# The end of a four-layer mixture-of-experts kernel: last LayerNorm and gates without Exp and Ln, gates of two batches at once, last experts placed between the batches' tails

## The chip, the cores and the metric

The kernel runs on one core of a Trainium2 chip, in one launch. The time is device microseconds from launch to end. Three runs are shown; beside them one execution was recorded by the hardware profiler, and all durations and positions below are from that one.

A core has TensorE (PE in the profile: matrix products, with weight loads shown apart as PEld), VectorE (DVE), ScalarE (ACT: activation functions, also copies), GpSimd (POOL), SyncE (SP, which here only starts transfers) and DMA queues. Each engine has its own list of instructions and waits for others by semaphores.

## The reference, cut to what matters

The input `x` is 4 batches of 512 tokens of 128 numbers. Four layers follow, each of an attention to a context of 32 tokens and a feed-forward part, each on a LayerNorm without gain. The change concerns the last feed-forward part (layer 3), and the LayerNorm ahead of it:

```python
def _L3_ffn_ref(x, router_w, w1, b1, w2, b2):
    TOP_K = 2
    xf = x.reshape(-1, D)
    logits = xf @ router_w.T                       # 8 experts
    probs = jax.nn.softmax(logits, axis=-1)
    top_v, top_i = jax.lax.top_k(probs, TOP_K)
    gates = top_v / (jnp.sum(top_v, axis=-1, keepdims=True) + 1e-09)
    out = jnp.zeros_like(xf)
    for e in range(E):
        ge = jnp.sum(jnp.where(top_i == e, gates, 0.0), axis=-1, keepdims=True)
        h = jax.nn.gelu(xf @ w1[e] + b1[e], approximate=False)
        out = out + ge * (h @ w2[e] + b2[e])
    return out.reshape(B, S, D)
...
x = x + _L3_xattn_ref(_layernorm(x, axis=-1), ctx_1024, mask_BxS2_ff1, ...)
x = x + _L3_ffn_ref(_layernorm(x, axis=-1), ...)
```

Every token goes through all 8 experts, weighted by its gates (zero for six of them). The hidden width is 256.

## The kernel before, in words

All data of the tail stays on the chip: `X[g]` is batch g, 128 partitions by 4 blocks of 128 numbers (block j holds tokens 128 j to 128 j + 127). Everything is float32. A product of 128 x 128 weights with 128 or 512 columns shows as two matmul records in the trace.

The program is written as Python generators, one chain for each batch. `together` (L110) starts the chains two steps apart and takes one step of each in turn, so that instructions of the batches are interleaved; a planner under it then orders what each engine gets by when it expects operands to be there. On the chip each engine works through that list.

The last stage, in `l3_ffn` (L1103 on), for each batch g:

1. `combine2(g)` (L1065, L1071) adds the outputs of layer 2's experts to `X[g]`.
2. `attend3(g)` normalises (`normed`, with its scaling on ACT, L219), transposes on PE (L233, the copy out of PSUM is L235), makes scores (L385), the maximum and the subtraction on DVE (L370, L371), the exponential on ACT (L372), a transpose (L398, its copy L400), the product with the values (L404), the division (L413, L414), and the output projection (L245), which is added to `X[g]` (L457). There are four blocks of scores a batch, 16 in all.
3. `route3(g)` (the chain in `routed`, L557) normalises `X[g]`: mean and variance on DVE (L192, L193), `v = variance + eps` (L195), `y = exp(-0.5 ln v)` on ACT (L197, L198), one Newton step on DVE (L202, L203, L205), the scaling on DVE (L223). Then come the transposes into `xnT[g]` (L233, L235), the product with the router's weights (L564) and the copy of the logits to SBUF (L570).
4. `gate(g)` finds the two largest logits (`argmax`, L582 to L589, twice), takes two exponentials on ACT (L1115, L1116) and makes the gates by small DVE operations (L1119 to L1131).

All chains run to their end first. Then a loop over the batches does the experts: the gates are transposed (L1138), copied (L1140) and multiplied with the second biases (L245, with `gT`), which is added to `X[g]`; for each of the 8 experts two hidden halves of 128 x 512 (L1146), Gelu on ACT (L1147), eight products back (L1151), and four DVE operations that add the gated result to `X[g]` (L1161). `X[g]` is then written out.

Hidden tiles `hT` have two buffers[...]. The tables of ACT's functions are loaded in sets: `exp_ln_tables` (L180) asks for one with Exp and Ln (L182); the load ahead of the Gelus is put in by the build (it shows at L1147). `fetch` loads this layer's weights early (L1230, L1231).

Of the kernel before, what the change touches and what calls it, by code (L numbers as in the profile page):

```python
# [8 lines left out]
F32 = mybir.dt.float32  # L9
# [58 lines left out]
def tile_kernel(ctx: ExitStack, tc: tile.TileContext, I, out):  # L68
# [115 lines left out]
        queued.close()  # L184
        queued.enter_context(tc.issue_after(load.ins))

    def moments(src, p=P, n=NJ):

        st = sm.tile([P, n, 6], F32, tag=f"st{n}", name="st")
        mv = sm.tile([P, n, 2], F32, tag=f"mv{n}", name="mv")  # L190
        for j in range(n):
            nc.vector.bn_stats(st[:p, j, :], src[:, j, :])  # L192
            nc.vector.bn_aggr(mv[:p, j, :], st[:p, j, :])  # L193
        v = small(n, "v")[:p]
        nc.vector.tensor_scalar(v, mv[:p, :, 1], EPS, None, ALU.add)  # L195
        y = small(n, "y")[:p]
        nc.scalar.activation(y, v, AF.Ln)  # L197
        nc.scalar.activation(y, y, AF.Exp, scale=-0.5)  # L198
        yield

        t = small(n, "t")[:p]
        nc.vector.tensor_tensor(t, y, y, ALU.mult)  # L202
        nc.vector.scalar_tensor_tensor(t, t, -0.5, v, ALU.mult, ALU.mult)  # L203
        r = small(n, "r")[:p]
        nc.vector.scalar_tensor_tensor(r, t, 1.5, y, ALU.add, ALU.mult)  # L205
        return mv[:p], r

    def normed(src, tag, plus=0.0, act=False, p=P, n=NJ, bufs=B, pool=wk):

        mv, r = yield from moments(src, p, n)  # L210
        y = pool.tile([P, n, D], F32, tag=tag, name=tag, bufs=bufs)
        if plus or act:
            c = small(n, "c")[:p]
            nc.vector.scalar_tensor_tensor(c, mv[:, :, 0], -1.0, r, ALU.mult, ALU.mult)
            if plus:
                nc.vector.tensor_scalar(c, c, plus, None, ALU.add)
        for j in range(n):
            if act:
                nc.scalar.activation(y[:p, j, :], src[:, j, :], AF.Identity, bias=c[:, j : j + 1], scale=r[:, j : j + 1])  # L219
            elif plus:  # L220
                nc.vector.tensor_scalar(y[:p, j, :], src[:, j, :], r[:, j : j + 1], c[:, j : j + 1], ALU.mult, ALU.add)
            else:
                nc.vector.tensor_scalar(  # L223
                    y[:p, j, :], src[:, j, :], mv[:, j, 0:1], r[:, j : j + 1], ALU.subtract, ALU.mult
                )
        yield
        return y
# [134 lines left out]
        nc.scalar.copy(vw[:rows], pt[:rows])  # L362
        return vw

    def softmax_terms(e, src, nh, n):

        e3 = e.rearrange("p (h n) -> p h n", n=n)
        src3 = src.rearrange("p (h n) -> p h n", n=n)
        mx = small(nh, "mx")
        nc.vector.tensor_reduce(mx, src3, AX.X, ALU.max)  # L370
        nc.vector.tensor_tensor(e3, src3, bc(mx, 2, n), ALU.subtract)  # L371
        nc.scalar.activation(e, e, AF.Exp)  # L372
        return e3

    def attend(xT, keys, values, g, H, n):
# [6 lines left out]
        for j0 in range(0, NJ, npb):  # L382
# [8 lines left out]
                )  # L391
            yield
            e = wk.tile([P, 512], F32, tag="att", name="att", bufs=B)
            softmax_terms(e, pt, npb * H, n)
            yield
            pt = psum()
            for k in range(4):
# [150 lines left out]
        return chain  # L548


    def routed(tag, w, bias=None, copies=()):


        xn, xnT = [None] * B, [None] * B
        logits = rk.tile([P, NT, NEXP], F32, tag=f"L{tag}", name="logits")

        def chain(g):  # L557
            xn[g] = yield from normed(X[g], "xn")
            for xd in copies:
                nc.sync.dma_start(xd[g * S : (g + 1) * S].rearrange("(j p) d -> p j d", p=P), xn[g])  # L560
            xnT[g] = yield from transposed(xn[g])
# [538 lines left out]
        return chain  # L1100


    def l3_ffn(xnT, logits, f3w1, f3w2, before, fetch):  # L1103
        gates = [None] * B

        def gate(g):
            L = logits[:, g * NJ : (g + 1) * NJ, :]
            m1, oh1 = argmax(L, NJ)
            m2, oh2 = argmax(without(L, oh1, NJ), NJ)

            z = rt.tile([P, NJ, NEXP], F32, tag="z", name="z", bufs=2)
            nc.vector.tensor_tensor(z, L, bc(m1, 2, NEXP), ALU.subtract)
            p2 = rt.tile([P, NJ], F32, tag="p2", name="p2", bufs=B)
            nc.vector.tensor_tensor(p2, m2, m1, ALU.subtract)
            nc.scalar.activation(z, z, AF.Exp)  # L1115
            nc.scalar.activation(p2, p2, AF.Exp)  # L1116
            yield
            p1 = rt.tile([P, NJ], F32, tag="p1", name="p1", bufs=B)
            nc.vector.tensor_reduce(p1, z, AX.X, ALU.add)  # L1119
            nc.vector.reciprocal(p1, p1)  # L1120
            nc.vector.tensor_tensor(p2, p2, p1, ALU.mult)
            den = rt.tile([P, NJ], F32, tag="den", name="den", bufs=2)
            nc.vector.scalar_tensor_tensor(den, p1, 1e-9, p2, ALU.add, ALU.add)
            nc.vector.reciprocal(den, den)
            nc.vector.tensor_tensor(p1, p1, den, ALU.mult)
            nc.vector.tensor_tensor(p2, p2, den, ALU.mult)
            gates[g] = rt.tile([P, NJ, NEXP], F32, tag="gates", name="gates", bufs=B)
            nc.vector.tensor_tensor(gates[g], oh1, bc(p1, 2, NEXP), ALU.mult)
            second = rt.tile([P, NJ, NEXP], F32, tag="second", name="second", bufs=2)
            nc.vector.tensor_tensor(second, oh2, bc(p2, 2, NEXP), ALU.mult)  # L1130
            nc.vector.tensor_tensor(gates[g], gates[g], second, ALU.add)  # L1131
            yield

        together([*(queue(before(g), gate(g)) for g in range(B)), fetch], 2)
        for g in range(B):
            pt = psum()
            for j in range(NJ):
                nc.tensor.transpose(pt[:NEXP, j * P : (j + 1) * P], gates[g][:, j, :], ident)  # L1138
            gT = ex.tile([NEXP, S], F32, tag="gT", name="gT", bufs=2)
            nc.scalar.copy(gT, pt[:NEXP])  # L1140
            add_to(X[g], proj(gT, f3b2, k=NEXP), X[g])
            for e in range(NEXP):
                hT = ex.tile([P, 2, S], F32, tag="hT", name="hT", bufs=2)
                for f in range(2):
                    pt = psum()
                    nc.tensor.matmul(pt, lhsT=f3w1[:, e, f * P : (f + 1) * P], rhs=xnT[g], start=True, stop=True)  # L1146
                    nc.scalar.activation(hT[:, f, :], pt, AF.Gelu, bias=col["f3_b1"][:, 2 * e + f : 2 * e + f + 1])  # L1147
                pt = psum().rearrange("p (j d) -> p j d", j=NJ)
                for j in range(NJ):
                    for f in range(2):  # L1150
                        nc.tensor.matmul(  # L1151
                            pt[:, j, :],
                            lhsT=hT[:, f, j * P : (j + 1) * P],
                            rhs=f3w2[:, e, f, :],
                            start=f == 0,
                            stop=f == 1,
                        )
                for j in range(NJ):
                    xj = X[g][:, j, :]
                    ge = gates[g][:, j, e : e + 1]  # L1160
                    nc.vector.scalar_tensor_tensor(xj, pt[:, j, :], ge, xj, ALU.mult, ALU.add)  # L1161
            nc.sync.dma_start(out[g].rearrange("(j p) d -> p j d", p=P), X[g])

    exp_ln_tables()
    xd0 = dram.tile([NTOK, D], F32, tag="xd0", name="xd0")
# [54 lines left out]
    with tc.tile_pool(name="lx", bufs=1) as lx:  # L1220
# [2 lines left out]
        attend3 = l3_xattn(*many3)  # L1223
        f3w1 = moe.tile([P, NEXP, 256], F32, tag="w1", name="f3w1")
        f3w2 = moe.tile([P, NEXP, 2, D], F32, tag="w2", name="f3w2")
        route3, _, xnT, L = routed(3, wide["router"])
        with tc.tile_pool(name="rt3", bufs=1) as rt, tc.tile_pool(name="ex3", bufs=1) as ex:

            def fetch():
# [1 line left out]
                nc.sync.dma_start(f3w2, I["f3_w2"].rearrange("e (c p) d -> p e c d", p=P))  # L1231
                yield

            l3_ffn(xnT, L, f3w1, f3w2, lambda g: queue(combine2(g), attend3(g), route3(g)), fetch())

# [168 lines left out]
```

## Time and profile before

| | us |
|---|---|
| median of 3 runs | 702.5 (698.09, 702.5, 703.27) |
| the profiled execution | 670.1 |
| its span, first to last instruction | 668.3 |

| engine | busy in the span |
|---|---|
| PE | 506.9 us (76%) |
| DVE | 330.6 us (49%) |
| ACT | 239.9 us (36%) |
| POOL | 164.3 us (25%) |

| stretch of the span | what runs |
|---|---|
| up to 456.5 us | layers 0 to 2 |
| 456.5 to 516.7 | adding layer 2's experts, layer 3's attention (last exponential ends 516.72) |
| 516.7 to 541.7 | last projections, last LayerNorm, router, gates |
| 541.7 to 668.3 | the 32 experts, writing out |

Timeline lines give start and duration in us, engine, line of the kernel, operation, what is written and read with shapes, how many instructions were merged into the line, and in brackets how long the engine stood idle before and who released it. In the table of stretches each engine has its busy time and number of instructions; PEclk is the granted clock of TensorE as a share of the full one. The chain of waits is the run of work that ended last, followed back from the end. Times of PE are partly modelled: matmuls overlap, and the end of one is an estimate.

### The profile page before, as it was taken

The page shows a single profiled execution, that of the slowest core. Times are in us where ns is not written, and L with a number is a line of the kernel's source. Part 1 is how long each engine was busy: PE and PEld are TensorE (multiplying, and loading weights), DVE is VectorE, ACT ScalarE, POOL GpSimd, SP SyncE. Part 2 cuts the span into 40 slices and gives each one's busy share as a digit, 9 for nine tenths or more (in the row PEclk, how much of TensorE's full clock was granted, in tenths as well). Part 3 has the DMA queues.
Part 4 walks back from the last instruction along what each step waited for, and adds up shares of the span by engine and source line. Part 5 has one row for each costly group of instructions (what it writes and reads, how often), then busy time and mean ns, then how long its engine had stood idle before and what let it go on. Part 6 is the DMA issues. An engine that isn't in the chain of part 4 may idle for free.

```text
span 668.3 us, 8842 instructions
## 1 busy us (share of the span) xinstructions
PE 506.9 (76%) x3047; PEld 387.0 (58%) x3047; DVE 330.6 (49%) x1378; ACT 239.9 (36%) x539; POOL 164.3 (25%) x203
## 2 busy tenths in 40 slices
PE   3658988425667968887635999950699699999996
PEld 2557765324655633676523887840377566776765
DVE  4686556352368740566681322115877843333322
ACT  2354655400225721334211333321555333333342
POOL 4244234304422100200006777772100000000000
PEclk9889989855958988997565999995799869999999
DMA  8900001291390007300202111345000000000000
GB/s 325 313 27 18 16 17 49 63 314 32 127 299 2 1 0 253 127 1 1 63 1 42 53 53 49 56 140 179 0 1 1 1 0 2 17 0 17 1 17 16
DMA packets 42990, 44.97 MB, mean 67 GB/s; under 512 B 5161, under 2 KB 31026, under 8 KB 42818
## 3 DMA queue, kind: packets, MB, share of 16 engines
q1 hardware_dynamic: 39442, 36.20, 16.5%
q0 software_dynamic: 3072, 6.30, 3.7%
q10 hardware_dynamic: 432, 1.92, 0.8%
q8 instruction: 24, 0.39, 0.2%
q14 instruction: 20, 0.16, 0.1%
HBM read 34.97 MB, written 9.44 MB: 66 GB/s over the span
## 4 chain that ended last, share of the span: by engine, by line
PE 48%; DVE 10%; POOL 7%; issue 6%; DMA 5%; ACT 4%; SPq 1%; POOLq 0%; DVEq 0%; ACTq 0%
PE pt L1151 9%; PE pt L1146 9%; PE pt L1037 4%; PE pt L1045 3%; POOL yd L689 3%; PE po L404 3%; PE pt L385 3%; PE pt L233 3%; DMA yd<-ye,to 2%; PE pt L916 2%; POOL xg L680 2%; PE pt L452 2%; PE pt L564 2%; PE pt L398 1%; PE pt L245 1%
## 5 line engine op out<-in xcount | busy, mean ns | idle before, releaser
L1151 PEld LDWEIGHTS pt<-f3w,hT 128*128 128x128 f32 x512 | 65.6, 191 | 33.4 <-ACT hT L1147 19.0
L1161 DVE SCALAR_TENSOR_TENSOR x<-pt,gates,x 128x128 f32<-128x128 f32 x128 | 36.0, 344 | 83.1 <-PE pt L1151 83.1
L1147 ACT ACTIVATE hT<-pt,cols 128x512 f32<-128x512 f32 x64 | 44.0, 688 | 73.8 <-PE pt L1146 73.5
L1151 PE MATMUL pt<-f3w,hT 128*128 128x128 f32 x512 | 68.2, 276 | 0.9 <-ACT hT L1147 0.6
L1146 PE MATMUL pt<-xnT,f3w 128*128 128x512 f32 x128 | 67.0, 612 | 0.0
L233 PE MATMUL pt<-cst,xn 128*128 128x128 f32 x96 | 25.0, 359 | 43.9 <-ACT xn L219 24.7
L680 POOL DMA_INDIRECT xg<-xd,inv x48 | 46.7, 972 | 44.5 <-DMA e_wg<-in_e_wg 16.4
L1040 ACT ACTIVATE hT<-pt 128x384 f32<-128x384 f32 (+1 forms) x64 | 27.9, 438 | 75.0 <-PE pt L1037 73.6
L689 POOL DMA_INDIRECT yd<-ye,to x48 | 46.9, 976 | 25.4 <-DVE ye L749 12.9
L233 PEld LDWEIGHTS pt<-cst,xn 128*128 128x128 f32 x96 | 15.3, 164 | 55.0 <-ACT xn L219 30.0
L192 DVE BATCH_NORM_STATS2 st<-x 128x6 f32<-128x128 f32 x128 | 32.3, 271 | 23.7 <-POOL x L545 17.6
L1045 PEld LDWEIGHTS pt<-f2w,hT 128*128 128x128 f32 x320 | 39.6, 191 | 3.3
L1037 PE MATMUL pt<-exT,f2w 128*128 128x256 f32 (+1 forms) x128 | 39.0, 448 | 2.6 <-DVE exT L713 2.6
L1045 PE MATMUL pt<-f2w,hT 128*128 128x128 f32 x320 | 40.4, 279 | 0.0
L235 ACT COPY xnT<-pt 128x512 f32<-128x512 f32 x40 | 23.2, 586 | 41.5 <-PE pt L233 41.1
L1052 DVE COPY ye<-pt 128x384 f32<-128x384 f32 (+1 forms) x16 | 7.9, 492 | 59.2 <-PE pt L1045 32.5
L398 PE MATMUL pt<-cst,att 128*128 128x128 f32 x128 | 20.5, 282 | 12.6 <-ACT att L372 12.6
L1037 PEld LDWEIGHTS pt<-exT,f2w 128*128 128x128 f32 x128 | 23.8, 197 | 10.7 <-DVE exT L713 2.8
L372 ACT ACTIVATE att<-att 128x512 f32<-128x512 f32 x32 | 20.0, 631 | 26.4 <-DVE att L371 26.1
L197 ACT ACTIVATE y<-v 128x4 f32<-128x4 f32 (+1 forms) x45 | 9.2, 203 | 53.5 <-DVE v L195 53.3
L385 PE MATMUL pt<-keys,xnT 128*128 128x256 f32 (+1 forms) x64 | 26.7, 523 | 0.9 <-ACT xnT L235 0.9
L370 DVE TENSOR_REDUCE mx<-pt 128x16 f32<-128x512 f32 (+1 forms) x32 | 21.7, 682 | 11.2 <-PE pt L385 11.0
(297 smaller groups left out, 1035.7 us busy)
## 6 DMA issues: line engine op xcount, KB each, us to landing
e_wg<-in_e_wg SPq DMA_DIRECT2D x8, 512.0 KB, 7.9
e_w<-in_e_w SPq DMA_DIRECT2D x8, 512.0 KB, 7.0
yg<-yd SPq DMA_DIRECT2D x12, 256.0 KB, 4.6
f0w<-in_f_w SPq DMA_DIRECT2D x1, 2048.0 KB, 13.2
yd<-zero SPq DMA_DIRECT2D x8, 256.0 KB, 3.4
ew<-in_e_w SPq DMA_DIRECT2D x8, 256.0 KB, 4.0
xd<-xn SPq DMA_DIRECT2D x8, 256.0 KB, 2.2
f2w<-in_f_w SPq DMA_DIRECT2D x1, 2048.0 KB, 8.3
```

What stands on the lines that cost most here:

```text
L192: nc.vector.bn_stats(st[:p, j, :], src[:, j, :])
L233: nc.tensor.transpose(pt[:, j * P : (j + 1) * P], src[:, j, :], ident)
L385: nc.tensor.matmul(pt[:, j * nk : (j + 1) * nk], lhsT=xT[:, (j0 + j) * P : (j0 + j + 1) * P], rhs=keys, start=True, stop=True,)
L680: nc.gpsimd.indirect_dma_start(out=dst, out_offset=None, in_=table[:], in_offset=bass.IndirectOffsetOnAxis(ap=idx, axis=0))
L689: ins = nc.gpsimd.indirect_dma_start(out=table[:], out_offset=bass.IndirectOffsetOnAxis(ap=to[:, c, e : e + 1], axis=0), in_=y, in_offset=None
L1037: nc.tensor.matmul(pt[:, : m * P], lhsT=f2w1[:, e, f * P : (f + 1) * P], rhs=xT, start=True, stop=True)
L1040: nc.scalar.activation(hT[:, f, : m * P], pt[:, : m * P], AF.Gelu)
L1045: nc.tensor.matmul(pt[:, c * D : (c + 1) * D], lhsT=hT[:, f, c * P : (c + 1) * P], rhs=f2w2[:, e, f, :], start=f == 0, stop=f == 3,)
L1146: nc.tensor.matmul(pt, lhsT=f3w1[:, e, f * P : (f + 1) * P], rhs=xnT[g], start=True, stop=True)
L1147: nc.scalar.activation(hT[:, f, :], pt, AF.Gelu, bias=col["f3_b1"][:, 2 * e + f : 2 * e + f + 1])
L1151: nc.tensor.matmul(pt[:, j, :], lhsT=hT[:, f, j * P : (j + 1) * P], rhs=f3w2[:, e, f, :], start=f == 0, stop=f == 1,)
L1161: nc.vector.scalar_tensor_tensor(xj, pt[:, j, :], ge, xj, ALU.mult, ALU.add)
```

## The change

- The LayerNorm in `route3` is called with `tables=False`: the first guess of the inverse root comes from an integer shift and subtraction on DVE, followed by three Newton steps in place of one. It is also called with `act=True`: the scaling is done on ACT, with a bias computed on DVE, instead of on DVE.
- `gate` works on two batches at once and waits until both have been routed. It takes one tanh in place of the two exponentials: exp(z) = (1 + t) / (1 - t) with t = tanh(z / 2).
- The table with Gelu (and tanh) is asked for once, by `after_exps`, which orders it behind the last attention exponential of every batch; tanh and Gelus are ordered behind it.
- The experts are a chain of their own, `experts()`, in the same `together` as the batches. It goes on once a batch's gates exist and all batches have left the attention. The bias product comes after the first expert of a batch instead of before it.

```diff
-    def moments(src, p=P, n=NJ):
+    def moments(src, p=P, n=NJ, tables=True):
...
-        y = small(n, "y")[:p]
-        nc.scalar.activation(y, v, AF.Ln)
-        nc.scalar.activation(y, y, AF.Exp, scale=-0.5)
-        yield
-
-        t = small(n, "t")[:p]
-        nc.vector.tensor_tensor(t, y, y, ALU.mult)
-        nc.vector.scalar_tensor_tensor(t, t, -0.5, v, ALU.mult, ALU.mult)
-        r = small(n, "r")[:p]
-        nc.vector.scalar_tensor_tensor(r, t, 1.5, y, ALU.add, ALU.mult)
+        if tables:
+            y = small(n, "y")[:p]
+            nc.scalar.activation(y, v, AF.Ln)
+            nc.scalar.activation(y, y, AF.Exp, scale=-0.5)
+            yield
+        else:
+
+            i = small(n, "i", I32)[:p]
+            nc.vector.tensor_scalar(i, v.bitcast(I32), 1, None, ALU.logical_shift_right)
+            nc.vector.tensor_scalar(i, i, -1.0, float(0x5F3759DF), ALU.mult, ALU.add)
+            y = i.bitcast(F32)
+
+        for _ in range(1 if tables else 3):
+            t = small(n, "t")[:p]
+            nc.vector.tensor_tensor(t, y, y, ALU.mult)
+            nc.vector.scalar_tensor_tensor(t, t, -0.5, v, ALU.mult, ALU.mult)
+            r = small(n, "r")[:p]
+            nc.vector.scalar_tensor_tensor(r, t, 1.5, y, ALU.add, ALU.mult)
+            y = r
...
-        nc.scalar.activation(e, e, AF.Exp)
+        exps[g] = nc.scalar.activation(e, e, AF.Exp)
...
-            xn[g] = yield from normed(X[g], "xn")
+            xn[g] = yield from normed(X[g], "xn", act=act, tables=tables)
...
+        def chain(g):
+            yield from before(g)
+            attended.append(g)
+            yield from route(g)
+            told.append(g)
+
+        def gate(g0):
+
+            while g0 + 1 not in told:
+                yield
+            n = 2 * NJ
+            L = logits[:, g0 * NJ : g0 * NJ + n, :]
+            m1, oh1 = argmax(L, n)
+            m2, oh2 = argmax(without(L, oh1, n), n)
...
+            nc.vector.tensor_tensor(z[:, :, :NEXP], L, bc(m1, 2, NEXP), ALU.subtract)
+            nc.vector.tensor_tensor(z[:, :, NEXP], m2, m1, ALU.subtract)
+            t = rt.tile([P, n, NEXP + 1], F32, tag="tanh", name="tanh", bufs=2)
+            with after_exps():
+                nc.scalar.activation(t, z, AF.Tanh, scale=0.5)
+            yield
+            nc.vector.tensor_scalar(z, t, -1.0, 1.0, ALU.mult, ALU.add)
+            nc.vector.reciprocal(z, z)
+            nc.vector.scalar_tensor_tensor(z, t, 1.0, z, ALU.add, ALU.mult)
...
+        def after_exps():
+
+            stack = ExitStack()
+            if not load:
+                with ExitStack() as behind:
+                    for g in range(B):
+                        behind.enter_context(tc.issue_after(exps[g].ins))
+                    load.append(nc.scalar.preload_act_table_set("gelu_and_others"))
+            stack.enter_context(tc.issue_after(load[0].ins))
+            return stack
...
+        def experts():
+            for g in range(B):
+                while gates[g] is None or len(attended) < B:
+                    yield
+                for e in range(NEXP):
+                    if e == 1:
+                        second_biases(g)
+                    expert(g, e)
+                    yield
+                nc.sync.dma_start(out[g].rearrange("(j p) d -> p j d", p=P), X[g])
+
+        together(
+            [*(chain(g) for g in range(B)), fetch, gate(0), gate(2), experts()],
+            late={g: 2 * g for g in range(B)} | {B: 2 * B, B + 1: 0, B + 2: 0, B + 3: 0},
+        )
...
-        route3, _, xnT, L = routed(3, wide["router"])
+        route3, _, xnT, L = routed(3, wide["router"], act=True, tables=False)
```

`expert(g, e)` and `second_biases(g)` hold the instructions of the old loop unchanged, with each Gelu issued under `after_exps()`.

## The prediction

> **What bounds the kernel now.** I read the page first (TensorE, PE, is busy 76% and holds 48% of the chain of waits; its two largest lines are the last experts, L1151 and L1146), then the busy time by stretch over the end, then the timeline of each engine between the last attention block and the first expert. Only that end is edited.
>
> ```profile
> core 0: us, PE busy (x) PEld busy (x) DVE busy (x) ACT busy (x) POOL busy (x), PEclk, DMA share, GB/s
> 514.60:528.20 13.60, 9.82 (x77) 8.51 (x75) 11.79 (x72) 4.58 (x13) 0.00 (x0) 1.00 0.00 1
> 528.20:541.70 13.50, 9.43 (x37) 7.21 (x37) 10.07 (x79) 3.93 (x12) 0.00 (x0) 0.50 0.00 1
> 541.70:548.20 6.50, 6.50 (x24) 3.78 (x24) 2.01 (x12) 2.73 (x4) 0.00 (x0) 0.72 0.00 0
> 548.20:668.30 120.10, 114.58 (x654) 81.19 (x652) 37.89 (x131) 43.59 (x64) 0.00 (x0) 1.00 0.03 10
> ```
>
> From 548.2 us on PE is full at full clock: 3.51 us for an expert (its blocks of 14 L1151 matmuls start at 553.53, 557.04 and 560.54 in the chain), 30.37 us for a batch. Nothing there changes. From 514.6 to 541.7 PE waits for a third of the time, and in the second half its clock (PEclk) is halved. The PE timeline of that part:
>
> ```profile
> 513.58 1.02 PE L385 MATMUL pt<-keys,xnT 128*128 128x512 f32 x2
> 514.44 1.05 PE L245 MATMUL pt<-w,oT 128*128 128x128 f32 x8
> 515.33 1.06 PE L404 MATMUL po<-v,aT 128*128 128x128 f32 x8
> 517.33 0.30 PE L233 MATMUL pt<-cst,xn 128*128 128x128 f32 x1 [0.94 <-DVE xn L223]
> ...
> 525.23 1.16 PE L245 MATMUL pt<-w,oT 128*128 128x128 f32 x8 [0.45 <-ACT oT L235]
> 528.52 1.15 PE L233 MATMUL pt<-cst,xn 128*128 128x128 f32 x4 [2.12 <-DVE xn L223]
> 530.34 2.08 PE L564 MATMUL pt<-w,xnT 128*128 128x128 f32 x8 [0.68 <-ACT xnT L235]
> ```
>
> Eight matmul records take 1.05 us before the clock drops and 2.08 us after. On ScalarE (ACT):
>
> ```profile
> 516.09 0.63 ACT L372 ACTIVATE att<-att 128x512 f32<-128x512 f32 x1 [1.33 <-DVE att L371]
> ...
> 540.86 0.21 ACT L1116 ACTIVATE p<-p 128x4 f32<-128x4 f32 x1 [1.09 <-DVE p L1114]
> 541.08 1.28 ACT L1147 ACT_TABLE_LOAD   x1
> 543.80 0.69 ACT L1147 ACTIVATE hT<-pt,cols 128x512 f32<-128x512 f32 x1 [1.44 <-PE pt L1146]
> ```
>
> The last attention exponential ends at 516.72, but 14 small exponentials and logarithms of this tail (0.2 us each) follow, so the Gelu table is loaded at 541.08. It costs nothing there: the first Gelu waits for PE.
>
> [...]
>
> **The change part by part.** Profiled execution: 670.1 us (span 668.3).
>
> *LayerNorm.* Per batch, Ln and Exp go (2 x 0.20 us on ACT); 2 integer operations, 6 more Newton steps and one bias (L214 kind) are added on VectorE (DVE), 0.15 us each. Dependent ones start 0.2 us apart (L1121, L1123, L1124 at 536.23, 536.45, 536.64), so the variance-to-scale chain goes from about 1.5 to 2.6 us. The scaling moves from DVE (4 in 1.06 us) to ACT (4 in 1.65 us, as the L219 row).
>
> *Gates.* Two batches at once: 4 x 23 small DVE operations become 2 x 26, 8 small activations become 2 tanh (some 0.26 us). It saves 40 x 0.1 us of DVE, but batch 0's gates now wait for batch 1's logits.
>
> *Table load.* It stands right behind the 16th exponential, 1.28 us, ahead of batch 0's scaling on ACT.
>
> *Order.* The program as built puts on PE: the last score matmul, then the transposes of batch 0's normed rows, and only between and behind these batch 1's output projection, the 15th value product, batch 0's router. Before, that projection and product ran at 514.44 to 516.39 and needed none of this. On DVE each batch's logits copy stands ahead of the next batch's whole norm. Of the experts, one (batch 0's first) lies ahead of batch 3's norm on PE and ACT. No DMA is added; SP's order and POOL's are the same.
>
> The walk, with rows above (PE at half clock 0.21 us a record in a dense stretch, 32 in 7.19 at L452; full 0.11):
>
> 1. Scores end 514.6; maximum, subtraction, exponential (0.69, 0.69, 0.63, with the new small ones between): 516.8. Load: 518.1. Scaling of batch 0: 518.1 to 519.75; first transpose 518.65. PE has stood 4.0 us, so I take its clock as halved (a 2.1 us pause in thin work, 526.4 to 528.5, did it before).
> 2. Transposes with batch 1's projection (12 records) to 521.5, 15th product to 523.2; clock back; router of batch 0 to 524.1. Before: 520.2.
> 3. Logits at 524.3, then 14 dependent DVE steps: batch 1's scale at 527.4, scaling to 529.05. PE meanwhile has 0.9 us of transposes and stands 3 us: half clock. Transposes and batch 2's projection to 530.5, 16th product to 532.2, router to 533.9. Before: 524.8.
> 4. Logits 534.2; 31 interleaved operations at 0.1 us, 3.4 in all: batch 2's scale at 537.6. Same pattern: router of batch 2 to 542.5. Before: 532.4.
> 5. First expert, 2 L1146 products, 3.2 us (1.7 full, 3.7 half clock): 545.7. Its Gelus end 546.5, then batch 3's scaling (its scale is ready at 546.2) to 548.2, beside PE's 16 L1151 records, to 548.2.
> 6. Transposes, gate transposes, copy, bias product: 550.4. Second expert to 554.5, with batch 3's router inside. Third to 559.1.
>
> Before, the third expert's last block ends at 553.53 + 1.56 = 555.1. From there on the order is the same, so the change costs 559.1 - 555.1 = **4.0 us**: 674.1 against 670.1. The median of the runs shown, 702.5, lies 32 above the profiled execution, for no reason that the trace shows; in proportion 4.0 becomes 4.2: **706.7, say 707**.
>
> The gain is there: an expert is done before batch 3's router. It is eaten by the three serial rounds of 9 us (before: 4.6, 7.6 and 5.7 from router to router), in which PE waits for DVE and then runs at half clock.
>
> **Unknown sizes.** [...] Spacing of dependent DVE operations over three chains of 14: 0.03 either way is 1.3 us. Clock at each round: the rivals. Integer shift and multiply: 0.14 us for a 128x16 int32 row (L631), so nothing else is hidden.
>
> **Rivals.**
> - *Half clock throughout* (slower). In 530 to 541 PE was busy more than half of the time and the clock stayed at 0.50. If that holds from 518 to 550, with 2.08 us for each group of eight, the walk puts the routers' ends at 526.1, 537.1 and 546.6 (rounds of 10 to 11 us) and the third expert's at 564.1: +9.0 us[...]. [...]
> - *Full clock throughout.* Routers end at 522.5, 529.9 and 537.4 (rounds of 7.4 us), the third expert at 553.2: -1.9, 700.6. For it: the clock survived pauses of 3 us at 36 to 39 and 206 to 209 us. Against: 4.0 us is longer.
> - *The overlap does what the words say* (faster). Tails keep the old pace, the first expert and the bias fill PE's pauses, and the second expert follows batch 3's router at 538.2: at half clock (3.7 + 1.7 us) it ends at 543.6 instead of 551.6 (the block at 550.03 + 1.56): -8, 694.5. It needs PE not to wait at 514.6, against the built order.
> - *It hardly overlaps at all.* The order shows one expert of 32 ahead of batch 3's router, so a gain of more than an expert and its cold start (541.7 to 548.1, 6.4 us, plus 2 for the bias) is excluded; this caps the rival above.
>
> **How the numbers follow.** Forecast 0.45, half clock 0.33, full clock 0.12, overlap 0.08, rest 0.02. One per cent is 7.0 us, about what runs from 698.09 to 703.27 can tell from no change. Forecast, own range +1.5 to +8 (704 to 711): a fifth beyond +7. Slower: 0.30 of the half-clock case, 0.09 of the forecast, 0.01: 0.40. Faster: 0.08. Within: 0.52. Range: 698 to 715, which leaves out the overlap and the ends of the others.
>
> **What would show it.** In the changed profile: the load right behind the last exponential near 517; PE idle some 4 us from 514.6, released by the scaled rows; PEclk 0.50 soon after; router to router about 9 us; the third expert's end near 559. Wrong if PE does not stand at 514.6, if rounds take under 7 us, or if any time moves ahead of 510 us, where no instruction changes.

## The result: 0.4% slower, and the profile after

| | kernel before | changed kernel |
|---|---|---|
| median of 20 runs each, us | 700.44 (695.71 to 703.27) | 703.20 (699.50 to 708.03) |
| ratio, 95% interval | | 1.0040 (1.0022 to 1.0059) |
| the profiled execution, us | 670.1 | 704.2 |
| its span, us | 668.3 | 702.4 |
| start of the last score product to start of the last block of expert products, us | 148.29 | 150.72 |

The change costs 2.8 us by the runs. The two profiled executions differ by 34 us, but 31.65 of these lie ahead of the last score product (513.58 us before, 545.23 after), where no instruction changed; the last section returns to that. I therefore compare the last row, called **the tail** from here on: two starts of the PE timeline subtracted (before: 661.87 - 513.58; after: 695.95 - 545.23). It grew by 2.43 us. To set a position of the changed kernel beside the prediction, take 31.65 off.

The table of stretches over the first three of the four parts shown before, each moved by 31.65 us:

```profile
core 0: us, PE busy (x) PEld busy (x) DVE busy (x) ACT busy (x) POOL busy (x), PEclk, DMA share, GB/s
546.25:559.85 13.60, 6.82 (x39) 6.33 (x39) 7.37 (x37) 6.01 (x12) 0.00 (x0) 0.75 0.00 0
559.85:573.35 13.50, 8.97 (x55) 8.00 (x55) 9.85 (x61) 4.53 (x11) 0.00 (x0) 0.75 0.00 1
573.35:579.85 6.50, 5.60 (x36) 3.85 (x35) 3.43 (x19) 4.08 (x8) 0.00 (x0) 1.00 0.01 3
```

In the first stretch PE is busy for 6.82 us instead of 9.82 and issues 39 records instead of 77. Its clock is worse than before (0.75 against 1.00). In the second and third the clock is better (0.75 and 1.00, against 0.50 and 0.72), and part of the loss comes back. The PE timeline shows where PE stands:

```profile
545.23 1.02 PE L396 MATMUL pt<-keys,xnT 128*128 128x512 f32 x2
550.37 0.86 PE L242 MATMUL pt<-cst,xn 128*128 128x128 f32 x2 [4.11 <-ACT xn L228]
551.02 0.64 PE L254 MATMUL pt<-w,oT 128*128 128x128 f32 x2
...
554.86 1.20 PE L575 MATMUL pt<-w,xnT 128*128 128x128 f32 x8
...
559.61 0.33 PE L242 MATMUL pt<-cst,xn 128*128 128x128 f32 x1 [2.67 <-ACT xn L228]
...
561.89 1.10 PE L575 MATMUL pt<-w,xnT 128*128 128x128 f32 x8
...
567.96 0.86 PE L242 MATMUL pt<-cst,xn 128*128 128x128 f32 x2 [4.53 <-ACT xn L228]
...
570.75 1.77 PE L575 MATMUL pt<-w,xnT 128*128 128x128 f32 x8
572.35 1.88 PE L1179 MATMUL pt<-xnT,f3w 128*128 128x512 f32 x4
```

Three pauses, of 4.11, 2.67 and 4.53 us, each ended by the scaled rows of a batch (`xn`, L228). The routers (L575) of batches 0 to 2 start at 554.86, 561.89 and 570.75: 7.0 and 8.9 us apart. Batch 1's output projection (L254, from 551.02) stands behind the first pause, though its operand `oT` had been copied by 545.59 (ACT L244, 545.00 + 0.59); before the change it started 0.86 us after the last score product. ScalarE shows what batch 0's rows waited for:

```profile
547.88 0.63 ACT L383 ACTIVATE att<-att 128x512 f32<-128x512 f32 x1 [1.80 <-DVE att L382]
548.52 1.28 ACT L1171 ACT_TABLE_LOAD   x1
549.82 1.65 ACT L228 ACTIVATE xn<-x,c,r 128x128 f32<-128x128 f32 x4
```

The last exponential, the load and the scaling follow each other without a gap.

### The profile page after: what moved, and what is told of

It reads as the page before. It is cut to its first block, busy times and chain, and to the rows that moved or that the text cites. A ratio compares the mean times of both kernels' runs of the same rounds, so it can differ in the third digit from the quotient of the medians.

```text
span 702.4 us, 8820 instructions
## 1 busy us (share of the span) xinstructions
PE 523.1 (74%) x3047; PEld 399.9 (57%) x3047; DVE 332.1 (47%) x1358; ACT 242.4 (35%) x541; POOL 164.2 (23%) x203
## 4 chain that ended last, share of the span: by engine, by line
PE 44%; DVE 12%; issue 7%; POOL 6%; ACT 4%; DMA 4%; another core or an unknown queue 3%; SPq 1%; POOLq 0%; DVEq 0%; ACTq 0%
PE pt L1185 8%; PE pt L1179 8%; POOL yd L700 4%; PE pt L1056 3%; PE pt L1048 3%; PE po L415 3%; PE pt L396 3%; PE pt L242 3%; PE pt L927 2%; DVE st L192 2%; POOL xg L691 2%; PE pt L865 2%; PE pt L463 1%; PE pt L409 1%
## 5 line engine op out<-in xcount | busy, mean ns | idle before, releaser
L1185 PE MATMUL pt<-f3w,hT 128*128 128x128 f32 x512 | 68.6, 277 | 1.3 <-ACT hT L1181 0.9
L1179 PE MATMUL pt<-xnT,f3w 128*128 128x512 f32 x128 | 64.9, 597 | 0.0
L242 PE MATMUL pt<-cst,xn 128*128 128x128 f32 x96 | 27.9, 382 | 45.5 <-ACT xn L228 31.1
L1051 ACT ACTIVATE hT<-pt 128x384 f32<-128x384 f32 (+1 forms) x64 | 26.4, 439 | 102.0 <-PE pt L1048 43.4
L1056 PE MATMUL pt<-f2w,hT 128*128 128x128 f32 x320 | 45.1, 296 | 21.9 <-ACT hT L1051 16.0
L1056 PEld LDWEIGHTS pt<-f2w,hT 128*128 128x128 f32 x320 | 42.7, 205 | 27.1 <-ACT hT L1051 17.0
L242 PEld LDWEIGHTS pt<-cst,xn 128*128 128x128 f32 x96 | 16.8, 180 | 58.5 <-ACT xn L228 37.0
L244 ACT COPY xnT<-pt 128x512 f32<-128x512 f32 x40 | 23.2, 585 | 43.7 <-PE pt L242 43.4
L409 PE MATMUL pt<-cst,att 128*128 128x128 f32 x128 | 22.1, 299 | 11.6 <-ACT att L383 11.6
L228 ACT ACTIVATE xn<-x,c,r 128x128 f32<-128x128 f32 x64 | 26.5, 483 | 11.1 <-DVE c L225 7.2
L396 PE MATMUL pt<-keys,xnT 128*128 128x256 f32 (+1 forms) x64 | 28.5, 554 | 0.9 <-ACT xnT L244 0.9
L415 PEld LDWEIGHTS po<-v,aT 128*128 128x128 f32 x192 | 26.2, 209 | 4.9 <-issue 3.3
```

The lines of the kernel that those rows point to most:

```text
L242: nc.tensor.transpose(pt[:, j * P : (j + 1) * P], src[:, j, :], ident)
L396: nc.tensor.matmul(pt[:, j * nk : (j + 1) * nk], lhsT=xT[:, (j0 + j) * P : (j0 + j + 1) * P], rhs=keys, start=True, stop=True,)
L415: nc.tensor.matmul(po[:, k, :], lhsT=aT[:, k * P : (k + 1) * P], rhs=of(values[k % nch], cols + hpc, g), start=True, stop=True,)
L1056: nc.tensor.matmul(pt[:, c * D : (c + 1) * D], lhsT=hT[:, f, c * P : (c + 1) * P], rhs=f2w2[:, e, f, :], start=f == 0, stop=f == 3,)
L1185: nc.tensor.matmul(pt[:, j, :], lhsT=hT[:, f, j * P : (j + 1) * P], rhs=f3w2[:, e, f, :], start=f == 0, stop=f == 1,)
```

## The experiments

The prediction's reason is that the order, not the work, costs the time: batch 1's projection was built in behind batch 0's transposes, which made the rounds serial. One difference in the code could do that. The old LayerNorm suspended its chain (`yield`) between Exp and the Newton step; the new branch has no such point, so that a batch's scaling and transposes are emitted one turn earlier, ahead of the next batch's projection. The rivals were the longer chain on VectorE, the half clock, ScalarE's scaling behind the table load, and the gates of two batches.

All runs together (the ratio is to the kernel before, run beside them):

| run | what differs | tail, us | PEclk | ratio (95% interval) |
|---|---|---|---|---|
| kernel before | | 148.29 | 0.83 | 1 |
| changed kernel | as in the result | 150.72 | 0.86 | 1.0040 (1.0022 to 1.0059) |
| after_again | the changed kernel again | 150.65 | 0.90 | 1.0038 (1.0015 to 1.0062) |
| yield_back | + suspension point | 145.42 | 0.93 | 0.9898 (0.9851 to 0.9946) |
| yield_back_2 | the same again | 145.33 | 0.93 | 0.9953 (0.9929 to 0.9977) |
| yield_dve | + suspension point, scaling on VectorE | 144.46 | 0.93 | 0.9950 (0.9923 to 0.9977) |
| dve_scale | scaling on VectorE | 148.64 | 0.93 | 1.0015 (0.9988 to 1.0042) |
| load_late | table load behind batch 0's scaling | 150.04 | 0.86 | 1.0014 (0.9987 to 1.0040) |
| newton2 | two Newton steps | 151.62 | 0.83 | 1.0046 (1.0021 to 1.0071) |
| experts_last | no early expert | 157.04 | 0.80 | 1.0110 (1.0066 to 1.0155) |
| gate_single | dve_scale with gates of one batch | 150.87 | 0.86 | 1.0050 (1.0028 to 1.0072) |
| ln_only | kernel before + new LayerNorm | 161.13 | 0.66 | 1.0191 (1.0146 to 1.0235) |
| ln_yield | ln_only + suspension point | 148.77 | 0.90 | 1.0032 (1.0012 to 1.0052) |
| early_yd | yield_dve, first products ahead of the gates | 144.58 | 0.93 | 0.9915 (0.9886 to 0.9944) |
| early_yd_2 | the same again | 145.57 | 0.90 | 0.9947 (0.9928 to 0.9967) |
| warm | spare products in two pauses | 149.07 | 0.97 | 1.0048 (1.0029 to 1.0068) |
| warm_n2 | warm with two Newton steps | 147.48 | 0.97 | 1.0018 (1.0001 to 1.0034) |
| warm_yd | yield_dve with spare products | 144.87 | 0.93 | 0.9927 (0.9901 to 0.9952) |

A tail is from one execution; a ratio is from many (6 runs of yield_back, ln_only and experts_last, 11 to 22 of the others). The experiments ran on three chips, each beside the kernel before on the same chip. PEclk is the mean over the first 50 us of the tail: 0.93 stands for 7 us of half clock, 0.86 for 14. It is no price by itself, since half clock costs nothing while PE stands: the changed kernel has 0.86 and 0.90 in its two profiles, and the same tail within 0.1 us. One per cent is 6.8 to 7.0 us.

### The suspension point put back

```diff
             y = i.bitcast(F32)
+            yield
```

> The changed kernel with one suspension point put back into the new LayerNorm, between the integer guess and the Newton steps, where the old one stood between Exp and its Newton step. No instruction is added or removed; the order on TensorE goes back to batch 1's output projection (and on to the 15th value product) ahead of batch 0's transposes. Theory A (the loss is the order: batch 1's projection waits behind batch 0's rows, which wait for the table load, so the rounds from router to router become serial): TensorE has work in the 4.1 us that it stands after the last score product, batch 1's norm no longer waits for batch 0, and the time is 4 to 7 us under the changed kernel's: 696 to 699, ratio to the kernel before 0.994 to 0.999. Theory B (the longer chain of dependent VectorE steps costs it, whatever the order): no more than 1 us off, 702 to 704, ratio 1.002 to 1.005. Theory C (the half clock after pauses costs it): pauses only move, 701 to 703.

The PE timeline of this run, to be read beside that of the changed kernel:

```profile
519.07 1.02 PE L397 MATMUL pt<-keys,xnT 128*128 128x512 f32 x2
519.93 1.05 PE L255 MATMUL pt<-w,oT 128*128 128x128 f32 x8
520.83 1.06 PE L416 MATMUL po<-v,aT 128*128 128x128 f32 x8
524.53 0.33 PE L243 MATMUL pt<-cst,xn 128*128 128x128 f32 x1 [2.65 <-ACT xn L229]
...
531.93 1.16 PE L576 MATMUL pt<-w,xnT 128*128 128x128 f32 x8
...
536.60 1.49 PE L243 MATMUL pt<-cst,xn 128*128 128x128 f32 x4 [2.62 <-ACT xn L229]
538.76 1.71 PE L576 MATMUL pt<-w,xnT 128*128 128x128 f32 x8 [0.68 <-ACT xnT L245]
```

Batch 1's projection and the 15th value product (L255, L416) are back ahead of batch 0's rows. Router 1 starts 12.86 us after the last score product instead of 16.66, router 2 19.69 instead of 25.52. The tail is 5.2 us shorter than that of the changed kernel (150.65), and the time goes from 0.4% above the kernel before to below it. Theory A holds, and B falls: nothing but the order of the same instructions was changed, and their numbers on each engine are equal. Part of the 5.2 us may come by way of the clock, which is at half for 7 us here instead of 10 and 14 in the two profiles of the changed kernel. But the clock alone, theory C, is not the loss: warm, below, has the order of the changed kernel and even less half clock (PEclk 0.97), and its tail is still 3.65 us longer than this one. The first ratio showed more than the tail can; the repeat took that back:

> The changed kernel with the suspension point put back, again, since its first ratio (0.9898) shows 4 us more than its tail (145.42 us, 2.87 less than the kernel before) accounts for. If the tail is all: tail 145.4, ratio 0.994 to 0.997. If something ahead of the tail differs too: ratio 0.988 to 0.992 again.

Tail 145.33, ratio 0.9953, as expected if the tail is all.

### The changed kernel on the chip of the first experiments

> The changed kernel itself, on the chip of the other experiments, so that they can be compared with it and not only with the kernel before. Its tail, from the start of the last score product to the start of the last block of expert products, took 150.72 us in its profile and 148.29 in that of the kernel before. Theory A (the order, in the tail alone): the same tail here within 0.3 us and +2.4 to +3 us in the times, ratio 1.002 to 1.005. Rival (part of the difference lies ahead of the tail, where no instruction changed): the ratio differs from that by more than 0.3 per cent.

Tail 150.65, ratio 1.0038. The loss lies in the tail.

### The new LayerNorm alone, without and with the point

```diff
-            xn[g] = yield from normed(X[g], "xn")
+            xn[g] = yield from normed(X[g], "xn", tables=False)
```

> The kernel before with the new LayerNorm alone (integer guess, three Newton steps, no suspension point), scaled on VectorE as before; gates, table load and experts as before. Theory A (order): its built order has the same serial rounds as the changed kernel and no early expert to give anything back, so it is slower than the changed kernel: +4 to +7 us against the kernel before, 704 to 707, ratio 1.006 to 1.010. Theory B (chain of steps alone): three rounds of about 1 us, less 0.4 us each for the two activations that go: +1 to +2 us, ratio 1.001 to 1.003. Theory D (the loss lies in ScalarE's scaling behind the table load, or in the gates of two batches): no loss here, -1 to 0 us.

It cost 12.8 us in the tail and 1.9% in the times, twice theory A's guess, which had left out that all rounds would run at half clock (PEclk is 0.50 from 3 to 10 us, from 13 to 20 and from 24 to 44 us, counted from the last score product). ln_yield adds the one `yield`:

> The kernel before with the new LayerNorm and its suspension point, scaled on VectorE; gates, table load and experts as before. It differs from the run with the new LayerNorm alone by that one point, so by the order, and from the kernel before by the 1.1 us longer chain and the two small activations that go. Tails so far: kernel before 148.29 us, new LayerNorm alone 161.13. Theory A (order): 149 to 151, ratio to the kernel before 1.001 to 1.004. Theory B (the chain carries the loss): over 154, ratio over 1.008.

148.77 us. One suspension point is worth 12.4 us here, with what it does to the clock (PEclk 0.90 instead of 0.66). The longer chain, less the two activations that go, costs 0.5 us by the tail and 2.2 by the times (0.32%). Theory B falls a second time.

With these, the change takes itself apart by tails, each of single executions: new LayerNorm in the old order +0.5 (148.29 to 148.77); gates of two batches, one table load, scaling on ScalarE and early expert -3.4 (to 145.42); the order that the missing point lets in +5.2 (to 150.65).

### No early expert

```diff
-            [*(chain(g) for g in range(B)), fetch, gate(0), gate(2), experts()],
+            [*(chain(g) for g in range(B)), fetch, gate(0), gate(2)],
...
+        run(experts())
```

> The changed kernel with all experts behind all tails instead of between them. Theory A: the one early expert and the bias fill pauses of TensorE and give back 3 to 5 us, so this is 3 to 5 us over the changed kernel: 706 to 708, ratio to the kernel before 1.008 to 1.012. Theory E (the early expert is in the way of batch 3's tail and gains nothing): 0 to -1 us against the changed kernel, 702 to 703, ratio 1.002 to 1.004.

6.4 us longer than the changed kernel by the tail, some 4.9 by the ratios (1.0110 and 1.0038); theory E falls. Up to router 2 it is alike to the changed kernel's first profile within 0.02 us (25.52 us after the last score product); then PE stands another 4.12 us for batch 3's rows. The overlap is real, and by the tail worth more than its one expert of 3.5 us.

### ScalarE's scaling, and the load

```diff
-        route3, _, xnT, L = routed(3, wide["router"], act=True, tables=False)
+        route3, _, xnT, L = routed(3, wide["router"], act=False, tables=False)
```

> The changed kernel with the rows scaled on VectorE (as in the kernel before) instead of ScalarE, so that batch 0's scaling is not queued behind the last attention exponential and the table load. The order on TensorE stays that of the changed kernel. Theory A: batch 0's rows come some 2.5 us earlier in the first round and the later rounds are 0.5 us shorter each or equal: 1.5 to 3 us under the changed kernel, 700 to 701.5, ratio to the kernel before 1.000 to 1.002; the TensorE pause after the last score product shrinks from 4.1 to under 2 us. Theory F (the scaling on ScalarE costs nothing, since something else ends the wait next): 0 to -0.5 us, ratio 1.003 to 1.005.

-2.0 us in the tail, the size that theory A gave, but not in its way: batch 0's rows came 0.76 us earlier, not 2.5, and the pause shrank from 4.11 only to 3.36 us. All three pauses together are 0.8 us shorter; most of the rest is work at a better clock (PEclk 0.93 instead of 0.86). Round 1 from transposes to router, for one, takes 3.85 us instead of 4.49. The ratios (1.0015 and 1.0038) have intervals that overlap. load_late leaves the scaling on ScalarE and moves the load:

```diff
                     for g in range(B):
                         behind.enter_context(tc.issue_after(exps[g].ins))
+                    behind.enter_context(tc.issue_after(scaled[NJ - 1].ins))
```

> The changed kernel with the table load moved behind batch 0's scaling on ScalarE instead of ahead of it; nothing else. Theory A: batch 0's rows come 1.28 us earlier, TensorE stands 2.8 us instead of 4.1, the load is hidden beside the transposes and batch 1's projection: tail 149.4 us, -1.3 us against the changed kernel. [...] Theory H (the load only moves in front of the copy of batch 0's transposed rows, and delays the router as much): 0.

-0.6 us in the tail, half of what theory A gave; the times can't tell it from the changed kernel. On ScalarE:

```profile
522.69 0.63 ACT L387 ACTIVATE att<-att 128x512 f32<-128x512 f32 x1 [1.80 <-DVE att L386]
524.14 1.65 ACT L230 ACTIVATE xn<-x,c,r 128x128 f32<-128x128 f32 x4 [0.82 <-DVE c L225]
525.80 1.28 ACT L1176 ACT_TABLE_LOAD   x1
```

With the load gone, the scaling waits 0.82 us for its bias `c` from VectorE. So of 1.28 us only some 0.5 were on the path: 4.10 us from the last score product to the scaling, against 4.59.

### Gates of two batches or of one

gate_single is dve_scale with `n = NJ`, one call of `gate` for each batch.

> The variant scaled on VectorE (tail 148.64 us), with the gates of one batch at a time, still by tanh. Theory A (VectorE's order is on the path in these rounds): 40 more small VectorE operations, of which about half stand in rounds 2 and 3 at 0.1 us each: tail 149.6 to 150.6. Rival J (waiting for two batches is what delays the early expert): tail 147 to 148.

2.2 us longer than dve_scale in the tail, 0.35% by the ratios, whose intervals overlap. Theory A's way shows in one round: the pause ahead of batch 1's rows, which VectorE ends, grew from 2.75 to 3.37 us. But the next one shrank from 4.40 to 3.94. The larger part is the clock (PEclk 0.86 instead of 0.93): round 2 takes 3.41 us from transposes to router instead of 2.25. So the two-batch gates are a gain in this execution; how much of it would stay at an equal clock was not tried.

### The chain's length and the clock

> The changed kernel with two Newton steps instead of three in the last LayerNorm, which changes its scale by some millionths. Theory A: three dependent steps of 0.2 us less in each chain, hidden for batch 0 behind the load and for batch 3 behind the early expert, so 0.6 us for batches 1 and 2 each: tail 149.5, -1.2 us. Theory B (the length of the chain is the loss): as much, and more where a shorter pause keeps the clock up: -1.8 to -3.

Neither: the tail is 1 us longer, and the times show no difference (1.0046 and 1.0038). The second pause did shrink by 0.6 us (2.67 to 2.08) and the third by nearly 1 (4.53 to 3.58), but the PE timeline of round 3 reads:

```profile
536.50 0.48 PE L242 MATMUL pt<-cst,xn 128*128 128x128 f32 x1 [3.58 <-ACT xn L228]
...
540.00 2.07 PE L575 MATMUL pt<-w,xnT 128*128 128x128 f32 x8 [0.67 <-ACT xnT L244]
541.86 3.62 PE L1179 MATMUL pt<-xnT,f3w 128*128 128x512 f32 x4
```

The router takes 2.07 us and the first expert's products 3.62, against 1.77 and 1.88 in the changed kernel: the half clock lasted until 30 us after the last score product instead of 27. Whether the clock is the term that decides here was then put to a test with spare products, whose results go nowhere:

```diff
+            if H == 16 and g == B - 1 and j0 == NJ - 1:
+                spare(xT, 4)
...
+        with tc.issue_after(last.ins):
+            spare(idle, k)
```

> The changed kernel with eight spare products of 128x512 on TensorE, whose results nobody reads: four behind the last score product, four behind the transposes of batch 3's attention rows, so that two of the three pauses (4.1 and 4.5 us) are filled. Everything else is as in the changed kernel. Theory L (half clock in rounds 1 and 3 costs as much as the records show): round 1 from transposes to router takes 2.3 us as in round 2 at full clock instead of 4.5, its router 0.1 less, round 3 1.4 us less and its router 0.7 less: -4.3 us, tail 146.4, ratio to the kernel before 0.995 to 0.999. Rival M (VectorE and ScalarE set the pace and only take over the wait): tail above 149, ratio over 1.001.

```profile
521.63 1.02 PE L403 MATMUL pt<-keys,xnT 128*128 128x512 f32 x2
522.50 3.60 PE L241 MATMUL pt<-xnT,cst 128*128 128x512 f32 x8
526.77 0.33 PE L247 MATMUL pt<-cst,xn 128*128 128x128 f32 x1 [0.68 <-ACT xn L228]
...
529.05 1.10 PE L584 MATMUL pt<-w,xnT 128*128 128x128 f32 x8
...
534.02 0.33 PE L247 MATMUL pt<-cst,xn 128*128 128x128 f32 x1 [2.99 <-ACT xn L228]
...
537.51 1.48 PE L584 MATMUL pt<-w,xnT 128*128 128x128 f32 x8
```

Round 1 takes 2.28 us from transposes to router, as expected (4.49 at half clock). But the clock then drops in round 2, 0.9 us behind the pause of 2.99 us that was left alone, and gives back 1.2 us (3.49 us from transposes to router). The tail is 1.6 us shorter in this execution, not 4.3, and the times show nothing (1.0048). These are the numbers that rival M gave (above 149, above 1.001), and theory L's size falls. But M's reason is not shown either: round 1 did get shorter, and what it gained went in part to the clock, which was kept over two pauses and dropped behind the third.

> The variant with spare products, with two Newton steps instead of three (the scale changes by some millionths). Theory L: with the clock kept, the shorter chain gains what the steps show, 0.6 us for each of batches 1 and 2: 1.2 us under the variant with spare products, tail 145.2, ratio 0.993 to 0.997. Rival N (two steps are no gain, the longer half clock was not why): the same tail as with three steps or longer.

147.48 us and 1.0018, not the 145.2 and 0.993 to 0.997 of theory L, but under warm by 1.6 us in the tail: at an equal PEclk of 0.97 the shorter chain gains about what its steps are worth, which it did not without the spare products. The times say less: the ratios differ by 0.3%, their intervals touch, and the medians (678.94 and 679.25 us) differ by 0.3 us. In its third round the records run at full clock (the router's eight take 1.16 us).

### Trying for the best version

> The variant with the suspension point put back, with the rows scaled on VectorE instead of ScalarE. Tail of that variant: 145.42 us. Theory A: batch 0's rows no longer wait for the load, TensorE's pause of 2.65 us ahead of them shrinks by 0.8 to 1 us, and batch 2's rows come 0.2 us earlier: tail 144.2 to 144.8, ratio to the kernel before 0.988 to 0.996. Rival I (VectorE has become the bound: its 1.06 us of scaling delays batch 1's norm): tail 145.4 to 146.5.

144.46 us: the size of theory A in the tail, though the pause shrank by 0.24 us only (2.65 to 2.41). In the times it cannot be told from yield_back_2 (0.9950 and 0.9953). Two additions to it:

> The variant with the suspension point put back and scaling on VectorE (tail 144.46 us), in which the first expert's products and Gelus no longer wait for the gates (only its last step, the weighted sum, does), so that they are built into the pause ahead of batch 2's rows. Theory A (TensorE pauses waiting for VectorE are what is left): 1.5 to 2.5 us of the 2.6 us pause are used, tail 142 to 143, ratio to the kernel before 0.990 to 0.993. Rival K (batch 2's transposes now stand behind the expert's products and delay router 2 and the gates as much as the pause gave): tail 144 to 145.5.

> The variant with the first expert's products ahead of the gates, again. Tail 144.58, the same as without (144.46), but ratio 0.9915 against 0.9950. If the tail is right: ratio 0.994 to 0.996 (-3.7 of 677 to 702 us is 0.9947). If it gains something that the tail does not hold: 0.990 to 0.993.

The repeat has 0.9947 and a tail of 145.57: no gain is left, which is rival K's size. The PE timeline of the repeat says why:

```profile
537.78 0.30 PE L243 MATMUL pt<-cst,xn 128*128 128x128 f32 x1 [2.61 <-DVE xn L233]
537.92 1.08 PE L1180 MATMUL pt<-xnT,f3w 128*128 128x512 f32 x2
...
545.88 0.60 PE L1203 MATMUL pt<-cst,gates 128*8 128x128 f32 x4 [0.90 <-DVE gates L1161]
```

The pause of 2.61 us is still there: the planner put the products behind the first transpose, not ahead of it. And now PE waits 0.90 us for the gates themselves.

> The variant with the suspension point put back and scaling on VectorE (tail 144.46 us, ratio 0.9950), with two spare products behind batch 3's output projection, in the pause of 2.6 us ahead of batch 2's rows. Theory L: router 2 and the first expert's products run at full clock, 1.0 and 0.75 us less: tail 142.7, ratio 0.991 to 0.994. Rival M: 144 to 145.

Tail 144.87, ratio 0.9927 (0.9901 to 0.9952). The tail speaks for rival M, the ratio for theory L, and its interval overlaps that of yield_dve. The trace holds both: in the stage with the spare products theory L's step came as forecast (router 2 takes 1.16 us instead of 2.07, the first expert's products 1.88 instead of 2.63), but round 1, ahead of them, was at half clock for 6.8 us instead of 3.4, and router 1 came 2.0 us later. Whether the two belong together stays open. The best that can be claimed is the changed kernel with the point put back: 0.5% faster than the kernel before (0.9953) and, over two chips, 0.85% faster than the change as it was made (1.0038).

## Why the prediction was right on the order and wrong on the clock of round 2

It forecast +4.0 us against the profiled execution, from a tail made serial by the built order. Measured: +2.4 in the tail, +2.8 by the runs. That the order is the cause is shown by yield_back and ln_yield, not only argued. Two steps failed. One is step 3, which took TensorE's clock as halved in round 2, where it stayed full (2.6 us too much). The other is the last one, which took a slowdown of 0.6% as one that runs can't tell from no change, where the runs show one of 0.4% clearly. When the clock drops and returns in these steps was the author's estimate; in the tail of before the trace shows one stretch at half clock, from 528.2 to 545.3 us. By the prediction's steps:

- **Step 1 (load in the path, PE stands 4.0 us): right.** Load to 518.15 (predicted 518.1), first transpose at 518.72 (518.65), pause 4.11 us. The step did not say what was late next: VectorE's bias is ready only 0.5 us before the load ends (549.12 + 0.17 against 549.80), so that moving the load gains no more (load_late). Nothing stood between the load and the scaling: the load ends at 548.52 + 1.28 = 549.80 and the scaling starts at 549.82.
- **Step 2 (half clock in round 1): right.** The half clock lasts from 548.3 to 555.2 us of the changed kernel, and router 0 ends at 524.4 (predicted 524.1).
- **Step 3 (half clock in round 2): the term that failed.** VectorE was right; the chain of dependent steps shows it:

```profile
556.48 0.17 DVE L195 TENSOR_SCALAR v<-mv 128x4 f32<-128x4 f32 x1
556.69 0.17 DVE L204 TENSOR_SCALAR i<-v 128x4 int32<-128x4 int32 x1
...
558.87 0.16 DVE L223 SCALAR_TENSOR_TENSOR c<-mv,r 128x4 f32<-128x4 f32 x1
```

  Steps are 0.20 us apart, and the scale is ready at 559.03 - 31.65 = 527.4 (predicted 527.4). But PE stood 2.67 us, not 3, and kept its clock until the next pause (halved from 565.4 on): transposes to router took 2.3 us at 0.11 us a record. Router 1 ended at 531.3 instead of 533.9: -2.6 us. The length of a pause does not decide this by itself. The two profiles of yield_back, one program, have a pause of 2.65 and 2.66 us ahead of batch 0's rows; behind it the clock was halved in the first (router 0 took 2.08 us) and kept in the second (1.16 us). So whether the step comes true may be luck in part.
- **Step 4: too short on VectorE.** The scale of batch 2 came at 567.38, 4.4 us after router 1's end, not 3.7:

```profile
566.44 0.60 DVE L1144 RECIPROCAL z<-z 128x72 f32<-128x72 f32 x1
566.95 0.10 DVE L213 SCALAR_TENSOR_TENSOR r<-t,r 128x4 f32<-128x4 f32 x1
567.07 0.23 DVE L1145 SCALAR_TENSOR_TENSOR z<-tanh,z 128x72 f32<-128x72 f32 x1
567.22 0.16 DVE L223 SCALAR_TENSOR_TENSOR c<-mv,r 128x4 f32<-128x4 f32 x1
```

  The reciprocal over 72 columns takes 0.60 us, where a multiplication of that size (L1145) takes 0.23; the prediction priced all 31 operations at 0.1. From router 1's end to router 2's the step took 9.5 us instead of 8.6: +0.9 us.
- **Step 5: too long.** The clock came back at 572.2 us, just before the first expert (572.35), whose products took 1.88 us instead of 3.2. -1.3 us. This too is a matter of where the half clock falls: in newton2 they took 3.62.
- **Step 6: too short.** From where PE leaves the first expert to the end of the bias product 3.1 us passed (576.68 to 579.78) instead of 2.2, since batch 3's rows and then the copy of the gates on ScalarE stand in between; the second expert, with batch 3's router inside, took 4.56 us instead of 4.1. +1.4 us.

These four (-2.6, +0.9, -1.3, +1.4) make the 1.6 us between +4.0 and +2.4; the largest is the clock of round 2. That errors of both signs cancel in part is luck too. The rivals: *half clock throughout* (+9.0) did not come, though ln_only, at half clock for 34 of the first 50 us, shows a loss of that kind (+12.8). *Full clock throughout* (-1.9) did not come either; what was said for it does not hold in the trace of before. The clock did not survive the pause at 36 to 39 us (3.32 us, ended at 38.39), but was halved from 40.1 on, less than 2 us behind it; and from 206 to 209 us PE worked for 1.2 us, with no pause above 1.6. *The overlap does what the words say* gave a tail 8 us shorter; with the point put back the tail is 2.9 shorter than before. The early expert was worth 6.4 in the changed kernel.

On the chances: +2.8 us lies within 1%, the case given the highest chance. But a difference of 0.4% was not beyond what can be told: 20 runs each put it between 0.2 and 0.6%. The bound of 7.0 us, taken from the spread of three runs, was too coarse, and the forecast of +0.6% should have been read as slower: this is the second step that failed.

With each window of 0.25 us weighted by its PEclk, the half clock lasts 6.8 and 6.8 us in the changed kernel, 6.8 and 3.4 in its second profile, and 10.2 in round 3 of newton2. What sets these lengths is not shown. One program can have the drop at different places: in the second profile of the changed kernel that of round 3 came 23.6 us after the last score product instead of 20.2, and the two profiles of yield_back differ over equal pauses, as step 3 says.

## What to carry to other kernels

Where a planner orders instructions from interleaved chains, a suspension point is part of the schedule: removing an operation together with the `yield` behind it moved a batch's transposes ahead of the next batch's projection and cost 5.2 us here, and 12.4 where the new LayerNorm was the only change. Compare the built order of each engine before and after, and put the point back before looking at the work. Where TensorE pauses in a tail as here (2.67 to 4.53 us in the changed kernel), read the clock beside every tail before putting a gain down to the edit (dve_scale, gate_single). Take a single profile's tail as one draw: two of the same program differ by 1.0 us (early_yd), so that many runs have to decide on differences of that size.

## What was not expected of the hardware

- **The same program in two lengths.** yield_back was profiled twice, with spans of 671.0 and 697.8 us; the tails differ by 0.1 us. The last score product came at 519.07 and 546.04. Between 400 and 480 us PE is busy for 68.6 us in the long profile, as in the first of the changed kernel (70.2), and for 55.4 in the short one, as in that of the kernel before (54.7): layer 2's experts, which nothing here changed, run later. In these runs the length went with the chip and not with the kernel: on two of the three chips of the experiments every run of the kernel before took 670 to 680 us, on the third 696 to 708, and the profile of 671.0 us is from one of the two, that of 697.8 from the third. The 32 us between the profiled 670.1 and the median of 702.5, which the prediction could not explain, would fit that if the profile came from another chip than the runs, which is not known. What makes one chip longer was not tried.
- **With two pauses filled, the clock dropped behind the third.** In warm this pause is 2.99 us long, and the clock is halved from 0.9 us behind it on; in the changed kernel it had been kept over one of 2.67. Whether the spare products have a part in that is not shown. Nor do these lengths make a threshold: one of 2.65 us was followed by half clock in the first profile of yield_back, and one of 2.66 us in its second was not.
